# Two cross attentions and an MLP in float32: order of side work, earlier operands, and weight loads of full width

## The chip, the core and the metric

The kernel runs on one core of a Trainium2 chip, as one launch. The metric is the device time in microseconds, from the start of the program to its end; lower is better. All data and all arithmetic are float32.

## The reference

The input x has 8 batches of 100 rows and 512 columns, and the context has 8 batches of 361 keys and 512 columns. A first attention with one head and weights of its own (here called layer 0) adds to x. Two cross attentions over the same context follow (l = 0 and 1 in the code), each with 16 heads of 128, biases, and one extra bias key and bias value. Then comes an MLP with 2048 hidden columns.

```python
def _cross_attention(q_in, kv_in, wq, bq, wk, bk, wv, bv, wo, bo, bias_k, bias_v):
    qh = (q_in @ wq + bq).reshape(b, q_len, H, K)
    kh = (kv_in @ wk + bk).reshape(b, t, H, K)
    vh = (kv_in @ wv + bv).reshape(b, t, H, K)
    kh = jnp.concatenate([kh, jnp.broadcast_to(bias_k, (b, 1, H, K))], axis=1)
    vh = jnp.concatenate([vh, jnp.broadcast_to(bias_v, (b, 1, H, K))], axis=1)
    logits = jnp.einsum('bqhk,bthk->bhqt', qh, kh) / scale
    weights = jax.nn.softmax(logits, axis=-1)
    ctx = jnp.einsum('bhqt,bthk->bqhk', weights, vh).reshape(b, q_len, H * K)
    return ctx @ wo + bo
...
x = res + _cross_attention(_layer_norm(x, ...), xf_1, ...)
...
return x + jax.nn.gelu(h @ w_fc1 + b_fc1, approximate=False) @ w_fc2 + b_fc2
```

## The kernel before, in words

**The algebra.** The keys are never formed. A head's queries are multiplied by the transposed key weights (`wide_queries`, L677), so that 16 heads of 100 rows make 1600 rows of 512 columns for each batch, in the tile `Z`. These rows are multiplied with the transposed context (scores), and the probabilities with the context itself (mixes); the value weights come after that (`head_out`, L881), and then the output weights (`attn_out`, L944). The big products use a scheme that needs seven block products instead of eight, at the price of sums of blocks that are formed beside them.

**Steps.** For each of the two attentions the batches go in pairs (q = 0 to 3), and the 1600 rows in three groups (g = 0 to 2). That makes 24 steps, and each has two halves, j = 0 and 1, one for each batch of the pair. In group 0 the first 64 rows are a tile of their own (`lone_tile`, L687 to L698); all other rows go in pairs of 128 row tiles (`pair_part`, L730, in four parts). Part 1 of a pair writes the score of the bias key into the probabilities on GpSimd (L755). The bias key's scores come from `bias_scores` (L627): four products of `E`, which has 16 columns for each block of 128 channels, with the normalised rows.

**What is formed beside the products.** `pair_sums` (L700 to L707) forms four sums of `Z` on GpSimd for one pair, in the tile `sums`, which has two buffers. VectorE transposes the probabilities in 32 by 32 blocks (`turned`, L354) into the tile `pT`, at a lower priority. When a group is turned, `column_sums` (L790) forms four sums of its blocks on GpSimd. The mixes (`mixed`, L831) use them so: blocks 0, 6 and 5 in part 0, blocks 7, 3 and 5 in part 1, blocks 1, 2 and 4 in part 2, blocks 8 and 4 in part 3. `bias_probs` (L866) fetches the probabilities of the bias key back from memory, broadcast to all partitions, into the tile `pb`, which has one buffer; `head_out` scales them on GpSimd (L878) and adds them on VectorE (L888). `weight_sums` (L903) forms sums of the output weights on GpSimd while l is 0 and q is odd. `bias_keys` (L606) makes `E` of the second attention while l is 0 and q is 2: two broadcasts by SP into a tile `h`, a subtraction on GpSimd (L611), and eight multiplications with accumulation on VectorE (L599) over the query weights. For the first attention the same is done in layer 0, with the VectorE instructions pinned to the program's order. The tile `h` has two buffers; the rows that are to be normalised (`load_rows`, L366, then L575) use it too.

**The order of the work.** A list of units is written out. Each step's score units, in groups, get a "fill" between them: projections for the next step, mixes of the half before, head products of the step before, output products, sums of weights. A unit names the weight blocks that it needs; rings of buffers (six slots in "w", two in "v") issue the loads by SP in the order of first use, as soon as the slot is free. A scheduler then gives every engine its queue, by the priority of the place in the list and by readiness in its own model of time; each engine runs its queue in order. `keep_in_program_order` keeps an instruction in its place.

The output units of a step begin with `bias_probs`, in the second half of the step after:

```python
res = [unit(lambda h=h: head_out(l, q, h), ("v", ("wv", l, q, h // 2))) for h in range(*WHOLE[g])]
return [unit(lambda: bias_probs(l, q, g))] + res
```

The sums for the next pair stand in part 1 of a pair (L1248), and the additions to the fill are these (L1287 to L1292):

```python
if l == 0 and q == 2:
    fill += e_units(1)[4 * k // 3 : 4 * (k + 1) // 3]
if l == 0 and q % 2:
    fill = woven(fill, sums_units(q // 2)[slice(*{0: (0, 2), 1: (2, 4), 2: (4, 6), 5: (6, 8)}.get(k, (0, 0)))])
if g == 1 and j and n < len(steps) - 2:
    fill.append(rows_unit((q + 1) % 4))
```

Of the kernel before, what the change touches and what calls it, by code (L numbers as in the profile page):

```python
# [18 lines left out]
P = 128  # L19
DT = D // P  # L20
# [59 lines left out]
def two_cross_attentions(ctx: ExitStack, tc: tile.TileContext, a: dict, out: bass.AP):  # L80
# [11 lines left out]
    def psum(pool, shape, name):  # L92
        return pool.tile(shape, F32, tag=pool.name, name=name)
# [110 lines left out]
    def unit(fn, *keys):  # L204
        return fn, keys
# [68 lines left out]
    ones = const.tile([P, 1], F32, tag="ones", name="ones")  # L274
    nc.gpsimd.memset(ones, 1.0)
    bqs = const.tile([P, 2, H], F32, tag="bqs", name="bqs")
    E = const.tile([P, 2, DT, H], F32, tag="E", name="E")
    e0 = const.tile([H, 2], F32, tag="e0", name="e0")
    half = const.tile([L, 1], F32, tag="half", name="half")
    nc.gpsimd.memset(half, -0.5)  # L280
# [313 lines left out]
    def bias_sums(l, p, dk, pinned):  # L594
        w = w4(("wqe", l, p))
        for c in range(DT):
            for h in range(2):
                wh = w[:, c, h * K : (h + 1) * K]
                ins = nc.vector.scalar_tensor_tensor(  # L599
                    wh, wh, 1.0 / math.sqrt(K), dk[:, h * K : (h + 1) * K], ALU.mult, ALU.mult,  # L600
                    accum_out=E[:, l, c, 2 * p + h : 2 * p + h + 1],
                )
                if pinned:
                    tc.keep_in_program_order(ins)

    def bias_keys(l, p):  # L606
        cols = slice(p * 2 * K, (p + 1) * 2 * K)
        dk = work.tile([P, 2, 2 * K], F32, tag="h", name=f"dk_{l}_{p}")
        broadcast(nc.sync, dk[:, 0, :], l, "bias_k", cols)
        broadcast(nc.sync, dk[:, 1, :], l, "bk", cols)  # L610
        nc.gpsimd.tensor_tensor(dk[:, 0, :], dk[:, 0, :], dk[:, 1, :], ALU.subtract)  # L611
        bias_sums(l, p, dk[:, 0, :], False)


    dk0 = [zf[:, i * 2048 : (i + 1) * 2048] for i in (3, 4)]
# [10 lines left out]

    def bias_scores(l, q):  # L627
        hT = hTs[l, q]
        ps = psum(ps_mm, [H, NQ], f"psb_{l}_{q}")
        for c in range(DT):  # L630
            nc.tensor.matmul(ps, E[:, l, c, :], hT[:, c, :], start=(c == 0), stop=(c == DT - 1))
        sT = work.tile([H, NQ], F32, tag="sT", name=f"sT_{l}_{q}", bufs=1)
        nc.vector.tensor_scalar(sT, ps, e0[:, l : l + 1], -1.0, ALU.add, ALU.mult)
# [65 lines left out]

# [90 lines left out]
    def column_sums(l, q, g, j, engine=nc.gpsimd):  # L790


        t, t3 = pTs[l, q, g, j], columns(l, q, g, j)
        nc.sync.dma_start(out=pbd[l, q * QB + j][:, slice(*ROWS[g])], in_=t3[TS : TS + 1, 2, :])
        engine.tensor_tensor(t[:, 6], t[:, 1], t[:, 0], ALU.subtract)  # L795
        engine.tensor_tensor(t[:, 1], t[:, 1], t[:, 3], ALU.subtract)
        engine.tensor_tensor(t[:, 7], t[:, 3], t[:, 6], ALU.subtract)  # L797
# [313 lines left out]
    W = "w"  # L1111
    steps = [(l, q, g) for l in range(2) for q in range(B // QB) for g in range(NG)]

    def e_units(l):

        return [unit(lambda p=p: bias_keys(l, p), (W, ("wqe", l, p))) for p in range(H // 2)]

    def project_units(n):
        l, q, g = steps[n]
# [30 lines left out]
    def out_units(n):  # L1150
        l, q, g = steps[n]
        res = [unit(lambda h=h: head_out(l, q, h), ("v", ("wv", l, q, h // 2))) for h in range(*WHOLE[g])]
        return [unit(lambda: bias_probs(l, q, g))] + res

    def rows_unit(q, tag="h"):

# [66 lines left out]
    def score_units(n, j):  # L1223
# [17 lines left out]
        for m, r in enumerate(pairs):  # L1241
            after = [r + 2 * P] if m == 0 else [pairs[0]] if j == 0 else []
            for part in range(4):
                u = [unit(lambda r=r, part=part: pair_part(l, q, j, r, part), key)]
                if part < 3:
                    n = (len(late) + 2 - part) // (3 - part)
                    u, late = late[:n] + u, late[n:]
                if part == 1:  # L1248
                    jj = j if m == 0 else j + 1
                    u += [unit(lambda x=x, jj=jj: pair_sums(l, q, jj, x)) for x in after]  # L1250
                res.append(u)
            late = end(r)
            res[-1], late = late[:1] + res[-1], late[1:]
# [5 lines left out]
    for n, (l, q, g) in enumerate(steps):  # L1259
        ahead = project_units(n + 1) if n + 1 < len(steps) else []  # L1260
        half_ahead = (len(ahead) + 1) // 2
        for j in range(QB):
# [10 lines left out]
            if n == len(steps) - 1:  # L1273
                outs = held[:4] if j == 0 else held[4:8]
            elif j and n:
                outs = out_units(n - 1)
                if n == len(steps) - 2:
                    held, outs = outs + out_units(n), []
            part = woven(part, outs) if len(part) > len(outs) else woven(outs, part)
            if mix:  # L1280
                lead = (len(part) + 2) // 3 if ahead else len(part) - 2 + j
# [3 lines left out]
            else:  # L1285
                fill += part
            if l == 0 and q == 2:  # L1287
                fill += e_units(1)[4 * k // 3 : 4 * (k + 1) // 3]
            if l == 0 and q % 2:
                fill = woven(fill, sums_units(q // 2)[slice(*{0: (0, 2), 1: (2, 4), 2: (4, 6), 5: (6, 8)}.get(k, (0, 0)))])  # L1290
            if g == 1 and j and n < len(steps) - 2:
                fill.append(rows_unit((q + 1) % 4))  # L1292
            groups = score_units(n, j)
            k = 0
            for i, us in enumerate(groups):
# [2 lines left out]
                units += fill[k:upto]  # L1298
                k = upto
    n = len(steps) - 1  # L1300
    drain = mix_units(n, 1) + out_units(n) + close_units(1, 1)
# [37 lines left out]
```

## Time and profile before

| What | us |
|---|---|
| Runs: median of 3 | 2037.32 |
| Runs: lowest and highest | 2035.34 and 2040.49 |
| The profiled execution: its time | 2032.83 |
| The profiled execution: its span | 2031.1 |
| TensorE clock granted, mean | 0.997 |
| Layer 0, 0 to 160 us: TensorE busy | 147.92 |
| First attention up to q = 2, 160 to 505 us: TensorE busy | 336.04 of 345 |
| q = 2 with E of the second attention, 505 to 730 us: TensorE busy | 217.17 of 225 |
| 730 to 1866 us: TensorE busy | 1112.92 of 1136 |
| The MLP, 1866 to 2031 us: TensorE busy | 157.44 of 165 |

An engine's busy time is the union of its instructions' records. TensorE has two rows: PE is the matmuls, PEld the loads of their stationary operand, which run beside the matmuls. In a row of the profile's timeline the first number is the start in us from the span's start, the second the duration, then the engine, the line, the operation, the tiles that are written and read, their shapes and how often in a row; in brackets is the engine's idle time before it and what ended that. The shape `128*64` of a load is rows by columns.

### The profile page before, as it was taken

The page shows a single profiled execution, that of the slowest core. Times are in us where ns is not written, and L with a number is a line of the kernel's source. Part 1 is how long each engine was busy: PE and PEld are TensorE (multiplying, and loading weights), DVE is VectorE, ACT ScalarE, POOL GpSimd, SP SyncE. Part 2 cuts the span into 40 slices and gives each one's busy share as a digit, 9 for nine tenths or more (in the row PEclk, how much of TensorE's full clock was granted, in tenths as well). Part 3 has the DMA queues.
Part 4 walks back from the last instruction along what each step waited for, and adds up shares of the span by engine and source line. Part 5 has one row for each costly group of instructions (what it writes and reads, how often), then busy time and mean ns, then how long its engine had stood idle before and what let it go on. Part 6 is the DMA issues. An engine that isn't in the chain of part 4 may idle for free.

```text
span 2031.1 us, 31457 instructions
## 1 busy us (share of the span) xinstructions
PE 1971.5 (97%) x10991; PEld 1799.4 (89%) x10991; DVE 1282.1 (63%) x3523; ACT 758.1 (37%) x2002; POOL 702.6 (35%) x1146
## 2 busy tenths in 40 slices
PE   9989999999999999999999999999999999999998
PEld 5668889998989888998999898989999999889998
DVE  2564766667666675666765765676666667665543
ACT  1324444444442334444432344444433444421231
POOL 3232432643344233444234323233243243325140
PEclk9999999999999999999999999999999999999999
DMA  8796224742645445534634353225334432135342
GB/s 253 255 313 201 83 80 134 219 135 75 195 125 159 135 125 185 180 105 128 205 117 130 114 169 111 94 73 170 97 114 128 133 124 82 56 105 167 116 128 71
DMA packets 250681, 283.87 MB, mean 140 GB/s; under 512 B 37608, under 2 KB 212108, under 8 KB 247196
## 3 DMA queue, kind: packets, MB, share of 16 engines
q1 hardware_dynamic: 246340, 271.51, 42.9%
q0 software_dynamic: 2112, 6.40, 0.9%
q10 hardware_dynamic: 2072, 3.97, 0.6%
q8 instruction: 87, 1.43, 0.3%
q14 instruction: 70, 0.57, 0.1%
HBM read 242.86 MB, written 38.97 MB: 139 GB/s over the span
## 4 chain that ended last, share of the span: by engine, by line
PE 75%; DVE 13%; ACT 4%; DMA 3%; POOL 2%; issue 2%; SPq 0%; DVEq 0%; POOLq 0%; ACTq 0%
PE sx L721 9%; PE mx L831 9%; PE pwo_P L944 7%; PE mz L831 7%; PE pq L661 7%; PE pqw L677 7%; DVE pT L354 6%; PE po L881 6%; PE sz L721 4%; PE my L831 3%; PE sy L721 2%; PE pfx L1084 2%; PE pgx L1035 2%; PE sc L474 2%; DVE wqe L599 2%
## 5 line engine op out<-in xcount | busy, mean ns | idle before, releaser
L354 DVE STREAM_TRANSPOSE pT<-p 32x192 f32<-32x192 f32 (+1 forms) x1664 | 602.2, 362 | 83.6 <-ACT p L338 53.7
L831 PE MATMUL mx<-pT,ctx 128*128 128x256 f32 (+3 forms) x960 | 283.0, 393 | 20.7 <-DVE Z L857 6.4
L721 PE MATMUL sx<-cT,Z 128*128 128x181 f32 x1152 | 230.0, 318 | 3.7 <-DVE p L761 3.7
L755 POOL TENSOR_SCALAR p<-nsb 128x1 f32<-128x1 f32 x192 | 37.4, 214 | 531.0 <-DVE pT L354 494.7
L831 PE MATMUL mz<-pT,ctx 105*128 105x256 f32 (+3 forms) x768 | 207.8, 393 | 9.5 <-POOL pT L795 8.4
L721 PEld LDWEIGHTS sx<-cT,Z 128*128 128x128 f32 x1152 | 195.2, 191 | 17.0 <-DVE p L761 5.6
L831 PEld LDWEIGHTS mx<-pT,ctx 128*128 128x128 f32 (+1 forms) x960 | 169.4, 190 | 44.2 <-POOL pT L797 9.5
L677 PE MATMUL pqw<-q,wkT 128*128 128x200 f32 x1024 | 195.6, 334 | 0.0
L881 PE MATMUL po<-Z,wv 128*128 128x200 f32 x1024 | 194.1, 333 | 1.6 <-DMA wv<-in_L_xattn_wv_dram 1.6
L661 PE MATMUL pq<-hT,wq 128*128 128x200 f32 x1024 | 193.7, 333 | 0.0
L775 ACT ACTIVATE p<-p,nm 128x362 f32<-128x362 f32 x192 | 114.8, 598 | 187.6 <-DVE nm L774 185.1
L677 PEld LDWEIGHTS pqw<-q,wkT 128*128 128x128 f32 x1024 | 177.5, 191 | 5.4 <-issue 0.5
L881 PEld LDWEIGHTS po<-Z,wv 128*128 128x128 f32 x1024 | 175.0, 190 | 7.4 <-DMA wv<-in_L_xattn_wv_dram 2.2
L831 PEld LDWEIGHTS mz<-pT,ctx 128*128 128x128 f32 (+1 forms) x768 | 143.8, 191 | 42.0 <-POOL pT L795 12.3
L661 PEld LDWEIGHTS pq<-hT,wq 128*128 128x128 f32 x1024 | 175.1, 190 | 4.2 <-issue 1.4
L774 DVE TENSOR_REDUCE nm<-p 128x1 f32<-128x362 f32 x192 | 101.5, 529 | 102.1 <-ACT p L766 92.2
L721 PE MATMUL sz<-cT,sums 128*128 128x181 f32 x768 | 150.2, 318 | 1.1 <-ACT p L749 1.1
L704 POOL TENSOR_TENSOR sums<-Z 128x256 f32<-128x256 f32 x96 | 69.8, 727 | 231.8 <-ACT Z L680 158.1
L680 ACT COPY Z<-pqw 128x400 f32<-128x400 f32 x256 | 122.3, 489 | 69.5 <-PE pqw L677 69.3
L338 ACT ACTIVATE p<-p,rden 128x362 f32<-128x362 f32 (+2 forms) x216 | 129.0, 599 | 34.6 <-DVE rden L337 34.6
L721 PEld LDWEIGHTS sz<-cT,sums 128*128 128x128 f32 x768 | 125.3, 190 | 1.7 <-ACT p L749 1.7
L831 PE MATMUL my<-pT,ctx 128*128 128x256 f32 (+3 forms) x384 | 102.5, 388 | 0.0
(379 smaller groups left out, 3112.6 us busy)
## 6 DMA issues: line engine op xcount, KB each, us to landing
wv<-in_L_xattn_wv_dram SPq DMA_DIRECT2D x64, 512.0 KB
wq<-in_L_xattn_wq_dram SPq DMA_DIRECT2D x64, 512.0 KB
wkT<-wkd SPq DMA_DIRECT2D x48, 512.0 KB
cT<-cTd SPq DMA_DIRECT2D x16, 1267.0 KB
wo_S<-wod SPq DMA_DIRECT2D x32, 512.0 KB
f<-in_L_xattn_w_fc_dram SPq DMA_DIRECT2D x32, 512.0 KB
wo_A<-in_L_xattn_wo_dram SPq DMA_DIRECT2D x24, 512.0 KB
xr<-xd SPq DMA_DIRECT2D x45, 200.0 KB
```

The costliest lines, as they stand in the source:

```text
L338: nc.scalar.mul(p[:rows, :n], p[:rows, :n], rden[:rows])
L354: nc.vector.transpose(dst[keys, :, :, i, :], src[i * QD : (i + 1) * QD, :, :, quarter, :])
L661: nc.tensor.matmul(ps, w[:, c, (h % 2) * K : (h % 2 + 1) * K], hTs[l, q][:, c, :], start=(c == 0), stop=(c == DT - 1),)
L677: nc.tensor.matmul(ps[:, c, :], w[:, h % 2, cc * P : (cc + 1) * P], qs[h], start=True, stop=True)
L680: nc.scalar.copy(Z[:, 2 * c2 : 2 * c2 + 2, :, h * L : (h + 1) * L], ps.rearrange("p c (b t) -> p c b t", b=QB),)
L704: nc.gpsimd.tensor_tensor(t[:, 0], a2[:, :2, :], a2[:, 2:, :], ALU.add)
L721: nc.tensor.matmul(ps[:, :KH], st["a"][a][:, c, :], st["ct"][:, blk, c, :], start=(first and c == 0), stop=(c == 1), skip_group_check=not ...
L774: nc.vector.tensor_reduce(nm, p[:, :S1], AX.X, ALU.max, negate=True)
L775: nc.scalar.activation(p[:, :S1], p[:, :S1], AF.Exp, bias=nm, accum_out=den)
L831: nc.tensor.matmul(ps, cx[:w, blk, :], pT[:w, u, :], start=first, stop=last, skip_group_check=more)
L881: nc.tensor.matmul(ps, w[:, c, (h % 2) * K : (h % 2 + 1) * K], Z[:, c, :, h * L : (h + 1) * L], start=(c == 0), stop=(c == DT - 1),)
L944: nc.tensor.matmul(ps, w[:, h, :], OB[i, j][:, h, :], start=(h == 0 and not more), stop=(h == 7), skip_group_check=more)
```

## The change

The parts are independent of each other in the code.

1. `E` becomes one row of 240 numbers for each partition: `E` of the second attention, `E` of the first, and zeros. A product of `bias_scores` loads 128 columns, the 16 wanted ones and what lies after them; only the first 16 rows of the result are read. A lone tile loads 128 columns of `Z` for 64, and only 64 rows of its result are read.
2. In `column_sums` the subtraction for block 7 comes before that for block 1.
3. `pair_sums` for the next pair stands in part 0 of a pair.
4. `bias_keys` is split: the two broadcasts (`bias_fetched`) are joined to a unit in the middle of the fill and name the weight block there; the subtraction and the VectorE sums stay at the fill's end, and the sums are pinned.
5. `bias_probs` is joined to a unit at three quarters of the fill of the step's first half, so it comes before the second half; the last two steps keep it where it was.
6. The two row loads are joined to a unit at three quarters of the fill.
7. Before the two sums of output weights in a fill stand two empty units that name the same weight blocks.

```diff
-    E = const.tile([P, 2, DT, H], F32, tag="E", name="E")
+    ef = const.tile([P, 2 * DT * H + P - H], F32, tag="E", name="E")
+    nc.gpsimd.memset(ef[:, 2 * DT * H :], 0.0)
+    E = [ef[:, (1 - l) * DT * H : (2 - l) * DT * H].rearrange("p (c h) -> p c h", c=DT) for l in range(2)]
...
-    def bias_keys(l, p):
+    dks = {}
+
+    def bias_fetched(l, p):
         cols = slice(p * 2 * K, (p + 1) * 2 * K)
-        dk = work.tile([P, 2, 2 * K], F32, tag="h", name=f"dk_{l}_{p}")
+        dks[p] = dk = work.tile([P, 2, 2 * K], F32, tag="h", name=f"dk_{l}_{p}")
         broadcast(nc.sync, dk[:, 0, :], l, "bias_k", cols)
         broadcast(nc.sync, dk[:, 1, :], l, "bk", cols)
+
+    def bias_keys(l, p):
+        dk = dks.pop(p)
         nc.gpsimd.tensor_tensor(dk[:, 0, :], dk[:, 0, :], dk[:, 1, :], ALU.subtract)
-        bias_sums(l, p, dk[:, 0, :], False)
+        bias_sums(l, p, dk[:, 0, :], True)
...
-        ps = psum(ps_mm, [H, NQ], f"psb_{l}_{q}")
+        ps = psum(ps_mm, [P, NQ], f"psb_{l}_{q}")
         for c in range(DT):
-            nc.tensor.matmul(ps, E[:, l, c, :], hT[:, c, :], start=(c == 0), stop=(c == DT - 1))
+            e = ef[:, ((1 - l) * DT + c) * H :][:, :P]
+            nc.tensor.matmul(ps, e, hT[:, c, :], start=(c == 0), stop=(c == DT - 1))
...
-        both = work.tile([P, 2, LONE], F32, tag="sums", name=f"both_{l}_{q}_{j}")
-        nc.gpsimd.tensor_tensor(both, Z[:, :2, j, :LONE], Z[:, 2:, j, :LONE], ALU.add)
+        both = work.tile([P, 2, P], F32, tag="sums", name=f"both_{l}_{q}_{j}")
+        nc.gpsimd.tensor_tensor(both, Z[:, :2, j, :P], Z[:, 2:, j, :P], ALU.add)
...
-        plain_scores(sc, rings["cT"].tiles["cT", l, q * QB + j], Z[:, :2, j, :LONE], Z[:, 2:, j, :LONE], both)
+        plain_scores(sc, rings["cT"].tiles["cT", l, q * QB + j], Z[:, :2, j, :P], Z[:, 2:, j, :P], both)
...
         engine.tensor_tensor(t[:, 6], t[:, 1], t[:, 0], ALU.subtract)
+        engine.tensor_tensor(t[:, 7], t[:, 3], t[:, 6], ALU.subtract)
         engine.tensor_tensor(t[:, 1], t[:, 1], t[:, 3], ALU.subtract)
-        engine.tensor_tensor(t[:, 7], t[:, 3], t[:, 6], ALU.subtract)
...
+    def sums_part(l, k):
+
+        n = {0: 0, 1: 1, 2: 2, 5: 3}.get(k)
+        if n is None:
+            return []
+        us = sums_units(l)[2 * n : 2 * n + 2]
+        return [unit(lambda: None, *us[0][1]), unit(lambda: None, *us[1][1])] + us
...
-                if part == 1:
+                if part == 0:
                     jj = j if m == 0 else j + 1
                     u += [unit(lambda x=x, jj=jj: pair_sums(l, q, jj, x)) for x in after]
...
-                fill += e_units(1)[4 * k // 3 : 4 * (k + 1) // 3]
+                for fetch, sums_ in e_units(1)[4 * k // 3 : 4 * (k + 1) // 3]:
+                    at = len(fill) // 2
+                    fill[at] = both_of(fill[at], fetch)
+                    fill.append(sums_)
...
+            if n and j == 0 and n < len(steps) - 1:
+                (fn, keys), (early, _) = fill[len(fill) * 3 // 4], probs_unit(n - 1)
+                fill[len(fill) * 3 // 4] = unit(lambda fn=fn, early=early: [fn(), early()], *keys)
             if g == 1 and j and n < len(steps) - 2:
-                fill.append(rows_unit((q + 1) % 4))
+                at = len(fill) * 3 // 4
+                fill[at] = both_of(fill[at], rows_unit((q + 1) % 4))
```

More of the change, by code (lines that the diff above doesn't have):

```diff
@@ L600, in bias_sums @@
                     wh, wh, 1.0 / math.sqrt(K), dk[:, h * K : (h + 1) * K], ALU.mult, ALU.mult,
-                    accum_out=E[:, l, c, 2 * p + h : 2 * p + h + 1],
+                    accum_out=E[l][:, c, 2 * p + h : 2 * p + h + 1],
                 )
@@ L628, in bias_scores @@
         hT = hTs[l, q]
-        ps = psum(ps_mm, [H, NQ], f"psb_{l}_{q}")
+        ps = psum(ps_mm, [P, NQ], f"psb_{l}_{q}")
         for c in range(DT):
-            nc.tensor.matmul(ps, E[:, l, c, :], hT[:, c, :], start=(c == 0), stop=(c == DT - 1))
+            e = ef[:, ((1 - l) * DT + c) * H :][:, :P]
+            nc.tensor.matmul(ps, e, hT[:, c, :], start=(c == 0), stop=(c == DT - 1))
         sT = work.tile([H, NQ], F32, tag="sT", name=f"sT_{l}_{q}", bufs=1)
-        nc.vector.tensor_scalar(sT, ps, e0[:, l : l + 1], -1.0, ALU.add, ALU.mult)
+        nc.vector.tensor_scalar(sT, ps[:H], e0[:, l : l + 1], -1.0, ALU.add, ALU.mult)
         nsb = work.tile([P, QB, 13], F32, tag="nsb", name=f"nsb_{l}_{q}")
@@ L1112, in two_cross_attentions, with both_of @@
     steps = [(l, q, g) for l in range(2) for q in range(B // QB) for g in range(NG)]
+    def both_of(u, v):
+        return unit(lambda: [u[0](), v[0]()], *(u[1] + v[1]))
     def e_units(l):
-        return [unit(lambda p=p: bias_keys(l, p), (W, ("wqe", l, p))) for p in range(H // 2)]
+        ks = [(W, ("wqe", l, p)) for p in range(H // 2)]
+        return [(unit(lambda p=p: bias_fetched(l, p), ks[p]), unit(lambda p=p: bias_keys(l, p), ks[p])) for p in range(H // 2)]
     def project_units(n):
@@ L1152, in out_units, with probs_unit @@
         res = [unit(lambda h=h: head_out(l, q, h), ("v", ("wv", l, q, h // 2))) for h in range(*WHOLE[g])]
-        return [unit(lambda: bias_probs(l, q, g))] + res
+        return [unit(lambda: None)] + res
+    def probs_unit(n):
+        l, q, g = steps[n]
+        return unit(lambda: bias_probs(l, q, g))
     def rows_unit(q, tag="h"):
@@ L1277, in two_cross_attentions @@
                 if n == len(steps) - 2:
-                    held, outs = outs + out_units(n), []
+                    held, outs = outs + [probs_unit(n)] + out_units(n)[1:], []
             part = woven(part, outs) if len(part) > len(outs) else woven(outs, part)
@@ L1287, in two_cross_attentions @@
             if l == 0 and q == 2:
-                fill += e_units(1)[4 * k // 3 : 4 * (k + 1) // 3]
+                for fetch, sums_ in e_units(1)[4 * k // 3 : 4 * (k + 1) // 3]:
+                    at = len(fill) // 2
+                    fill[at] = both_of(fill[at], fetch)
+                    fill.append(sums_)
             if l == 0 and q % 2:
-                fill = woven(fill, sums_units(q // 2)[slice(*{0: (0, 2), 1: (2, 4), 2: (4, 6), 5: (6, 8)}.get(k, (0, 0)))])
+                fill = woven(fill, sums_part(q // 2, k))
+            if n and j == 0 and n < len(steps) - 1:
+                (fn, keys), (early, _) = fill[len(fill) * 3 // 4], probs_unit(n - 1)
+                fill[len(fill) * 3 // 4] = unit(lambda fn=fn, early=early: [fn(), early()], *keys)
             if g == 1 and j and n < len(steps) - 2:
-                fill.append(rows_unit((q + 1) % 4))
+                at = len(fill) * 3 // 4
+                fill[at] = both_of(fill[at], rows_unit((q + 1) % 4))
             groups = score_units(n, j)
@@ L1300, in two_cross_attentions @@
     n = len(steps) - 1
-    drain = mix_units(n, 1) + out_units(n) + close_units(1, 1)
+    drain = mix_units(n, 1) + [probs_unit(n)] + out_units(n)[1:] + close_units(1, 1)
     norm, hid, mlp, end = mlp_units(0)
```

## The prediction

> **What bounds the kernel now.** I read the page's parts 1 and 2 first, then who waited for whom on TensorE, then the trace in order of time around each long wait. Part 1:
>
> ```profile
> PE 1971.5 (97%) x10991; PEld 1799.4 (89%) x10991; DVE 1282.1 (63%) x3523; ACT 758.1 (37%) x2002; POOL 702.6 (35%) x1146
> ```
>
> TensorE is the bound in every stage; nothing else is over 63%. So the change can only win time in which TensorE stands still or runs slowly. As the ends of matmuls are modelled, I took start to start times of neighbours: 154 ns for 181 columns, 169 for 200, 216 for 256, 242 for 288. What lies above these, summed over all 10,991 records (a matmul of this kernel is two of them), is about 86 us: 17 in layer 0, some 70 after it. That is all there is to win. The waits, of TensorE alone (total, times, longest):
>
> ```profile
> PE mz L831 <- POOL pT L795: 8.4, 9, 1.7
> PE mx L831 <- DVE Z L857: 6.4, 7, 2.0
> PE mx L831 <- ACT Z L840: 6.3, 4, 2.7
> PE mx L831 <- POOL pT L797: 5.3, 7, 0.9
> ```
>
> Two of the four are column_sums on GpSimd. Around 297 us it looks like this:
>
> ```profile
> 296.62 0.72 POOL L795 TENSOR_TENSOR pT<-pT 128x256 f32<-128x256 f32 x1 [0.85 <-DVE pT L354]
> 297.30 0.73 POOL L704 TENSOR_TENSOR sums<-Z 128x256 f32<-128x256 f32 x1
> 297.99 0.73 POOL L796 TENSOR_TENSOR pT<-pT 128x256 f32<-128x256 f32 x1
> 298.67 0.73 POOL L797 TENSOR_TENSOR pT<-pT 128x256 f32<-128x256 f32 x1
> ```
>
> TensorE wants block 7 (L797) second, but GpSimd makes block 1 (L796) before it and a pair sum (L704) between. The third place is the layer's second half, 505 to 760 us, where E of layer 1 is formed on VectorE:
>
> ```profile
> 569.57 0.29 DVE L599 SCALAR_TENSOR_TENSOR wqe<-wqe,dk 128x128 f32<-128x128 f32 x1 [5.34 <-DMA wqe<-in_L_xattn_wq_dram]
> ```
> ```profile
> 570.60 0.88 PE L721 MATMUL sx<-cT,Z 128*128 128x181 f32 x4 [1.65 <-DVE p L761]
> ...
> 575.05 1.74 PE L831 MATMUL mx<-pT,ctx 128*128 128x256 f32 x4 [1.95 <-DVE Z L857]
> ```
>
> VectorE stands 5.34 us before weights that haven't landed, with L761 and L857 queued behind; TensorE stands twice for it. And then its clock drops (the stretch, its length, PE busy, clock):
>
> ```profile
> 575.40:578.80 3.40, 3.40 (x12) 0.50 0.23 82
> 579.00:583.00 4.00, 4.00 (x24) 1.00 0.42 112
> 708.50:711.90 3.40, 3.40 (x11) 0.50 0.67 237
> ```
>
> Twelve matmuls in 3.4 us against 24 in 4.0. Last, the narrow weights (weight loads of one lone tile):
>
> ```profile
> 175.18 1.73 PEld L474 LDWEIGHTS sc<-cT,Z 128*64 128x64 f32 x12 [0.24 <-issue]
> ...
> 177.79 0.61 PEld L721 LDWEIGHTS sx<-cT,Z 128*128 128x128 f32 x4 [0.26 <-issue]
> ```
>
> The load isn't run ahead of the matmuls before it, on entering the 64 columns and on leaving them, and no semaphore is named.
>
> **What the Trainium skill says.** "TensorEngine Tiling (Array Packing)", Key Properties: "Changing tiling mode (not just tile) drains the TensorE"; its Available Configurations have column tiles of 64 and 32. The trace agrees: at 53 borders between a load of 64 or 16 columns and one of 128 the next matmul starts 86 to 95 ns late, and at the 100 column loads of layer 0 it doesn't. "TensorE: Matmul & The Clock Gate", What's actually happening: an idle window of about 3.4 us halves the clock; the trace has three such windows of 3.41 us inside the span, two of them right after these waits. The same page's table of specifications calls VectorE's and GpSimd's queues strict FIFO: L761 behind L599 above is that.
>
> **The change, part by part.**
>
> *Wide weights.* bias_scores loads 128 columns for 16, lone tiles 128 for 64. 53 borders of 91 ns vanish: **-4.8 us**, all on the path. Added: loads of 190 ns for 136 and 96. The rows sx (128 columns) and sc (64) both go at 153 to 154 ns per matmul, so they cost nothing while a matmul of 181 or 200 columns runs beside them. "both" (L694) grows from 454 to the 727 ns of L704, 16 x 0.27 = 4.4 us of GpSimd, which idles 65%; sc wants it only after twelve records (1.8 us). Without that cover at most 4.4 us. The zero fill at the start lies in GpSimd's 38 us wait. Bounds: 0 (if the pause isn't the width) to -4.8.
>
> *Block 7 before block 1.* L797 moves up by one operation, 0.69 us from start to start. TensorE's excess put down to L797 is 6.8 us in 11 places: one each of 1.08 (269 us), 1.07 (299), 1.08 (498), 1.07 (929), 1.07 (1353), 0.5 (1730), 0.5 (1816) and four of about 0.1. Taking up to 0.69 from each: 5 x 0.69 + 2 x 0.5 + 0.4 = 4.9. What is late next is block 1 (M3), 0.69 us behind block 7; M2 and the two z products stand between, six records of 0.216, 1.3 us, so it isn't late. Where the pair sum goes out of the way as well, the rest goes too. I take **-4.9**; bounds -3.5 and -6.8.
>
> *Pair sums at part 0.* L704 to L707 (2.9 us of GpSimd) go ahead of the two L755, which wait for VectorE's transposes 72 times, 494.7 us in all. At 206 us L755 waits 7.22 us, then three sums run, then L795, and TensorE loses 1.19 us: that goes. At 722 (1.25) and 1728 (1.86) the first sum waits for ScalarE's copy of Z, which this edit doesn't hasten; at 239, 297, 496, 926 and 1351 L795 itself waits for transposes. Queued behind the sums now: L755 and column_sums, if Z isn't copied yet. **-1.2**; bounds -4 and +3.
>
> *Layer 1's E (bias_fetched, bias_keys).* Sixteen broadcasts and eight weight loads of SP are asked for half a fill (some 15 us) earlier; eight GpSimd subtractions (0.73) and 64 VectorE sums stay, at the fill's end and pinned. The wait at 569 cost 1.81 + 2.11 + 0.15, plus half of a 3.41 us window, 1.7: 5.8. The burst of L599 at 703 to 706 cost 2.84 + 1.7 = 4.5; bursts at 740 to 760 1.5. The row loads' wait (4.24 us of VectorE at 765, 3.4 of TensorE) hangs on a free buffer, and I leave it. The first goes, half of the others: **-8**; bounds -12 and +10 (the third rival).
>
> *Rows, bias probabilities and output weights earlier.* Rows: two loads of 200 KB in SP's queue a quarter of a fill earlier. Probabilities: GpSimd's 42.7 us of waits for pb go, save the last two (9.9, 4.1), which aren't moved; but no long wait of TensorE that I followed back passes through L878, so 0. The two loads now sit in SP's queue before wq, wkT and wv; should pb's single buffer not be free, these wait too (SP waited 68.3 us for L888 in 13 places). Weight sums: 24.1 us of GpSimd waits go, and a wor block holds one of six weight slots half a fill longer; TensorE waits for no wq, wkT or wo now, and its worst wait for wv is 0.8 us. **0** for the three; bounds -2 and +3.
>
> Sum: 4.8 + 4.9 + 1.2 + 8 = 18.9. The order of the queues is made anew by a scheduler, so other queues meet elsewhere; of some 70 us of waits a twentieth, 3.5 us, may come back. **-15.4 us**. The profiled execution took 2032.8 us (span 2031.1, 1.7 around it), the median of the runs is 2037.3; a saving on TensorE holds for both, so I take it from the median: **2022 us**, and a profile near 2018.
>
> **The rivals.**
>
> *The waits come back elsewhere.* Only widths and block order count (9.7), and moved sums and bursts cost 5 to 6: **2033 us**. For it: VectorE has 1282 us of work, and most long waits end in a run of transposes; against it: the 5.34 us wait is for a load alone.
>
> *The pause isn't the width.* Then 4.8 stays: **2027 us**. For it speaks only that "issue" is named, not a cause; against it the 100 column loads, which show none.
>
> *Slower: pinned sums hold VectorE.* Eight groups of L599 now stand at a fixed place, behind GpSimd's subtraction, which stands behind L755. One such wait of 5.34 us costs TensorE 3.9 us (1.81 + 2.11). Eight cost 31, less the 8.4 that today's sums cost (3.4 of lost clock apart) and 10.9 of the other parts: +12, **2049 us**. It decides from five groups on (19.6 against 19.3). Against it: the fetch is half a fill ahead, and GpSimd waited at most 4.95 us for a broadcast just issued.
>
> *All of it works*, the interleaved sums and the row loads too: 4.8 + 6.8 + 1.2 + 11.8 + 3.4 = 28, **2009 us**.
>
> **How the numbers follow.** Chances: forecast 0.52, waits come back 0.20, width 0.08, slower 0.07, all 0.13. A measurement tells about 0.3% (6 us) from no change. Faster than 2031: the forecast, all, width, and a third of the second, 0.80; slower than 2043: 0.06; the rest 0.14. The range 2008 to 2035 reaches from the best case to the waits that come back, and leaves out the slower case and the tails of these two.
>
> **What would show it.** Loads of 64 and 16 columns gone and no pause of 91 ns around sc and psb; L797 waits under 2 us; no half clock at 575 and 708; VectorE never over 2 us before L599. Wrong would be: VectorE idle before L599 on the subtraction, new waits of sx or mx on L761 or L857, or TensorE waiting for wq or wkT loads.

## The result, and the profile after

| What | us |
|---|---|
| Before: median of 5 runs | 2037.32 |
| After: median of 5 runs | 2016.07 |
| After: lowest and highest | 2015.62 and 2020.65 |
| After, the profiled execution: time and span | 2018.84 and 2017.0 |

The ratio of after to before is 0.9906, with a 95% interval of 0.9892 to 0.9921: 19 us less (16 to 22). The ratio isn't the quotient of the two medians, which lie 21.3 us apart; where the two differ I use the ratio. The two profiled executions lie 14.0 us apart (2032.83 and 2018.84), their spans 14.1. The lines of the kernel after have moved: L354 is L358 now, L599 is L603, L721 is L731, L755 is L765, L761 is L771, L795 to L797 are L805 to L807 (block 7 at L806, block 1 at L807), L831 is L841, L840 is L850, L857 is L867, L575 is L579.

Part 1 of the page of after:

```profile
PE 1963.9 (97%) x10991; PEld 1814.2 (90%) x10991; DVE 1276.8 (63%) x3523; ACT 757.4 (38%) x2002; POOL 707.2 (35%) x1147
```

The work of the engines is the same to 1%, so what was won is time in which TensorE stood or ran slowly. Who waited for whom on TensorE after (total, times, longest):

```profile
PE mx L841 <- DVE Z L867: 6.6, 7, 2.1
...
PE mz L841 <- POOL pT L805: 4.9, 6, 1.0
...
PE ph L582 <- DVE xr L579: 4.0, 1, 4.0
...
PE mx L841 <- ACT Z L850: 2.3, 2, 1.6
...
PE mx L841 <- POOL pT L806: 1.2, 5, 0.3
```

Block 7 went from 5.3 to 1.2 us, the first sum (L805) from 8.4 to 4.9, ScalarE's copy of Z (L850) from 6.3 to 2.3. VectorE's Z (L867) is unchanged at 6.6 against 6.4, and a row is new: ph, the transposes of normalised rows, waits once, 4.0 us. GpSimd around the place that was shown at 297 us, in the trace of after:

```profile
294.40 0.73 POOL L805 TENSOR_TENSOR pT<-pT 128x256 f32<-128x256 f32 x1
295.09 0.34 POOL L765 TENSOR_SCALAR p<-nsb 128x1 f32<-128x1 f32 x2
295.39 0.73 POOL L806 TENSOR_TENSOR pT<-pT 128x256 f32<-128x256 f32 x1
296.07 0.73 POOL L807 TENSOR_TENSOR pT<-pT 128x256 f32<-128x256 f32 x1
```

Between the first sum (L805) and block 7 (L806) stand only two short writes of the bias key's score (L765); the pair sums have gone ahead of both. The weight loads of the lone tile at 175 us:

```profile
175.42 1.90 PEld L478 LDWEIGHTS sc<-cT,Z 128*128 128x128 f32 x12
...
177.90 0.65 PEld L731 LDWEIGHTS sx<-cT,Z 128*128 128x128 f32 x4
```

128 columns, and the idle time in brackets is gone on entering and on leaving. VectorE's sums for E between 500 and 800 us (the group's busy time, the mean of one, the idle time before):

```profile
L603 DVE SCALAR_TENSOR_TENSOR wqe<-wqe,dk 128x128 f32<-128x128 f32 x64 | 18.0, 345 | 0.2
```

VectorE waits 0.2 us before them in all, where it waited 11.0 for the 64 sums of before. The clock, at the place of 575 us and at two new ones (a half clock is a stretch in which TensorE is granted half of its full clock; the columns are stretch, its length, PE, PEld, DVE, ACT and POOL busy, clock, DMA share and GB/s):

```profile
575.40:578.80 3.40, 3.40 (x20) 3.13 (x19) 1.85 (x5) 2.30 (x7) 0.00 (x0) 1.00 0.43 114
692.50:695.90 3.40, 3.40 (x11) 3.14 (x10) 3.22 (x9) 0.37 (x1) 0.71 (x3) 0.50 0.24 82
...
713.00:716.40 3.40, 3.40 (x12) 3.04 (x13) 1.34 (x4) 0.37 (x1) 3.32 (x6) 0.50 0.65 196
```

The half clock at 575 is gone; the one at 708 has become two, each behind a stand of TensorE, a time without a matmul (2.1 us before the first, 4.0 before the second). The second stand is the new row of the waits. On TensorE, VectorE and SP it looks like this:

```profile
708.27 0.62 PE L841 MATMUL mx<-pT,ctx 128*128 128x256 f32 x2
712.87 0.70 PE L582 MATMUL ph<-ident,xr 100*128 100x100 f32 x3 [3.98 <-DVE xr L579]
```
```profile
708.79 0.08 DVE L603 DVE_READ_ACCUMULATOR wqe<-wqe,dk 128x1 f32 x1
...
712.27 0.55 DVE L579 TENSOR_SCALAR xr<-xr,mv,rstd 100x512 f32<-100x512 f32 x1 [0.69 <-DVE pT L358]
```
```profile
708.93 0.31 SPq L370 DMA_DIRECT2D xr<-xd  x1
```

The row load leaves 0.06 us after the last sum for E has been read out (708.79 + 0.08): both use the tile `h`, and the pinned sums kept its buffer. The load and seven transposes follow, then L579, and TensorE has the transposes of these rows next in its queue.

Where the time went, by what TensorE's start to start times lie above those without a wait (the measure of the prediction; all excesses over 30 ns, the half clock in the rows where it falls; the prediction put the total of before at about 86, by this count it is 91.8):

| Cause, by the lines of before | before, us | after, us |
|---|---|---|
| borders of 64, 16 and 128 columns | 4.8 | 0 |
| mx on block 7 (L797) | 6.8 | 2.0 |
| mz on the first sum (L795) | 9.9 | 5.9 |
| mx on ScalarE's Z (L840) | 7.0 | 2.7 |
| mx on VectorE's Z (L857) | 8.5 | 9.2 |
| sx on VectorE's p (L761) | 4.5 | 4.1 |
| sx on ScalarE's p (L746) | 4.4 | 6.8 |
| mz on ScalarE's Z (L843) | 2.4 | 5.3 |
| ph on VectorE's rows (L575) | 0 | 4.1 |
| sc on ScalarE's cT, in layer 0 | 0 | 4.0 |
| pd on ScalarE's xc, in layer 0 | 4.6 | 1.5 |
| all causes, these and smaller ones | 91.8 | 78.0 |

The total falls by 13.8, near the 14.1 between the spans. In layer 0, which the change hardly touches, one wait went and another of like size came (the last two rows of causes).

### The profile page after: what moved, and what is told of

Its sections match the earlier page's. It is cut to its first block, busy times and chain, and to the rows that moved or that the text cites. A ratio compares the mean times of both kernels' runs of the same rounds, so it can differ in the third digit from the quotient of the medians.

```text
span 2017.0 us, 31494 instructions
## 1 busy us (share of the span) xinstructions
PE 1963.9 (97%) x10991; PEld 1814.2 (90%) x10991; DVE 1276.8 (63%) x3523; ACT 757.4 (38%) x2002; POOL 707.2 (35%) x1147
## 4 chain that ended last, share of the span: by engine, by line
PE 79%; DVE 10%; DMA 4%; ACT 3%; issue 2%; POOL 1%; SPq 0%; DVEq 0%; ACTq 0%; POOLq 0%
PE sx L731 9%; PE mx L841 9%; PE mz L841 7%; PE pq L671 7%; PE pqw L687 7%; PE po L891 7%; PE pwo_P L954 6%; DVE pT L358 5%; PE sz L731 5%; PE my L841 3%; PE sc L478 2%; PE sy L731 2%; PE pfx L1094 2%; PE pgx L1045 2%; DMA xr<-xd 1%
## 5 line engine op out<-in xcount | busy, mean ns | idle before, releaser
L358 DVE STREAM_TRANSPOSE pT<-p 32x192 f32<-32x192 f32 (+1 forms) x1664 | 602.1, 362 | 84.3 <-ACT p L342 54.5
L841 PE MATMUL mx<-pT,ctx 128*128 128x256 f32 (+3 forms) x960 | 281.3, 391 | 11.2 <-DVE Z L867 6.6
L731 PE MATMUL sx<-cT,Z 128*128 128x181 f32 x1152 | 229.6, 318 | 3.2 <-DVE p L771 3.1
L841 PE MATMUL mz<-pT,ctx 105*128 105x256 f32 (+3 forms) x768 | 208.3, 393 | 7.3 <-POOL pT L805 4.9
L731 PEld LDWEIGHTS sx<-cT,Z 128*128 128x128 f32 x1152 | 195.2, 191 | 16.6 <-DVE p L771 5.2
L765 POOL TENSOR_SCALAR p<-nsb 128x1 f32<-128x1 f32 x192 | 39.1, 223 | 477.6 <-DVE pT L358 421.4
L841 PEld LDWEIGHTS mx<-pT,ctx 128*128 128x128 f32 (+1 forms) x960 | 170.0, 190 | 30.6 <-DVE Z L867 6.8
L841 PEld LDWEIGHTS mz<-pT,ctx 128*128 128x128 f32 (+1 forms) x768 | 144.0, 191 | 40.9 <-ACT Z L853 8.1
L731 PE MATMUL sz<-cT,sums 128*128 128x181 f32 x768 | 149.3, 316 | 0.7 <-ACT p L759 0.7
L731 PEld LDWEIGHTS sz<-cT,sums 128*128 128x128 f32 x768 | 124.8, 189 | 1.0 <-ACT p L759 1.0
L841 PE MATMUL my<-pT,ctx 128*128 128x256 f32 (+3 forms) x384 | 102.5, 388 | 0.0
```

Of the source, the lines that this page charges most:

```text
L358: nc.vector.transpose(dst[keys, :, :, i, :], src[i * QD : (i + 1) * QD, :, :, quarter, :])
L731: nc.tensor.matmul(ps[:, :KH], st["a"][a][:, c, :], st["ct"][:, blk, c, :], start=(first and c == 0), stop=(c == 1), skip_group_check=not ...
L841: nc.tensor.matmul(ps, cx[:w, blk, :], pT[:w, u, :], start=first, stop=last, skip_group_check=more)
```

## The experiments

The parts have the numbers that they have in the section on the change. Each kernel was run in turn with the kernel before; a ratio is to that, with its 95% interval. Beside the ratio I set the two traces against each other by steps: how much earlier or later than in the trace of before each of the 24 steps starts. That tells where a part wins or loses, which one sum of a profile doesn't, since half clocks fall in other places from one execution to the next. A step starts with the first score product of its first pair; in the trace of before the steps of q = 2 (6 to 8) start at 558, 628 and 717 us, step 9 at 791 and step 10 at 859 us. (The row for 505 to 730 us in the table ahead of the prediction covers q = 2 only roughly.)

**Part 1 alone.**

```diff
-        ps = psum(ps_mm, [H, NQ], f"psb_{l}_{q}")
+        ps = psum(ps_mm, [P, NQ], f"psb_{l}_{q}")
...
-        both = work.tile([P, 2, LONE], F32, tag="sums", name=f"both_{l}_{q}_{j}")
+        both = work.tile([P, 2, P], F32, tag="sums", name=f"both_{l}_{q}_{j}")
```

> The kernel before with the wide weights alone (part 1). Theory, the pause is the switch of the load's width: all 53 pauses of about 91 ns around sc and psb vanish and nothing else changes, 4.8 us less, a ratio of 0.9976. Rival, the pause is not the width: the pauses stay, ratio 1.000. Second rival, the scheduler makes other queues of it: the pauses go, but other waits of TensorE change by more than 2 us.

Measured: 2032.66 against 2035.51 us, ratio 0.9982 [0.9973, 0.9991], so 3.7 us. In its trace no excess is left at a border. Its span, 2032.8, shows no gain; this execution has five half clocks where the one of before has three, and at 1.7 us each the two explain 3.4 of the 5.4 us that are missing against the ratio. The pause is the width.

**Part 2 alone.**

```diff
         engine.tensor_tensor(t[:, 6], t[:, 1], t[:, 0], ALU.subtract)
+        engine.tensor_tensor(t[:, 7], t[:, 3], t[:, 6], ALU.subtract)
         engine.tensor_tensor(t[:, 1], t[:, 1], t[:, 3], ALU.subtract)
-        engine.tensor_tensor(t[:, 7], t[:, 3], t[:, 6], ALU.subtract)
```

> The kernel before with block 7 formed before block 1 alone (part 2). Theory: TensorE's excess at L797's place falls from 6.8 to about 1.9 us (what a pair sum between the two leaves), 4.9 us less, a ratio of 0.9976. Rival: block 1 is late next or the wait moves to the next mix, so that the ratio is within 0.999 to 1.001 though the wait at block 7 is gone.

Measured: 2031.4 against 2035.51, ratio 0.9978 [0.9971, 0.9986], 4.5 us. The excess at block 7 fell from 6.8 to 2.0, and no wait for block 1 came up in its place.

**Part 3 alone.**

```diff
-                if part == 1:
+                if part == 0:
```

> The kernel before with the pair sums in part 0 alone (part 3). Theory: the wait at 209 us (1.2 us) goes and little else moves, ratio about 0.9994. Rival: the sums, now ahead of L755 and of the column sums, hold these up: waits on L795 and on ScalarE's copies grow by 3 us or more, ratio 1.0015.

Measured: 2032.37 against 2035.51, ratio 0.9987 [0.9978, 0.9995], 2.6 us. The excess at the first sum (L795) fell from 9.9 to 7.9: the wait of 1.19 us behind the sums of 206 us is gone, and the one at 1728 fell from 1.85 to 1.14.

**Part 4 alone.**

```diff
-                fill += e_units(1)[4 * k // 3 : 4 * (k + 1) // 3]
+                for fetch, sums_ in e_units(1)[4 * k // 3 : 4 * (k + 1) // 3]:
+                    at = len(fill) // 2
+                    fill[at] = both_of(fill[at], fetch)
+                    fill.append(sums_)
```

> The kernel before with the split bias keys alone (part 4). Theory: the 5.3 us wait of VectorE at 569 us and the half clock after it go, the stretch from 505 to 630 us is 6 us shorter; then the row load that shares the buffers h waits for the pinned sums, and a stall of some 4 us with a half clock appears near 710 us, so that about 2 to 6 us stay, ratio 0.997 to 0.999. Rival, the pin itself holds VectorE: it stands before L599 for over 2 us in several of the eight groups and the ratio is above 1.

Measured: 2044.36 against 2035.51, ratio 1.0043 [1.003, 1.0056]: **slower** by 8.7 us. By steps, it wins 6.3 us between 558 and 628 us (the wait for weights at 569 is gone, as the forecast said) and loses 13.8 between 791 and 859. Of the stall that the forecast had near 710 a stand of 3.6 us came, at 720, but it ended with column sums on GpSimd (L800) and not with the rows, and from step 7 to step 9 the kernel gains 0.4 us all the same. In the place of the loss TensorE stands twice:

```profile
816.78 1.57 PE L726 MATMUL sx<-cT,Z 128*128 128x181 f32 x4 [4.01 <-DVE p L766]
826.83 2.07 PE L836 MATMUL mx<-pT,ctx 128*128 128x256 f32 x4 [5.58 <-DVE Z L862]
```

and each stand has a half clock with it, the first from 816.7 us on for 3.4 us, the other from 823.5 on for 6.8 (same columns as above):

```profile
816.50:819.90 3.40, 3.12 (x9) 2.76 (x10) 1.51 (x5) 1.80 (x5) 2.62 (x8) 0.53 0.83 244
...
823.50:830.30 6.80, 3.47 (x9) 2.65 (x10) 3.97 (x11) 1.96 (x6) 2.06 (x3) 0.50 0.54 160
```

VectorE's own waits from 787 to 830 us name the cause, the rows of layer 1's first pair:

```profile
DVE xr L575 <- DMA xr<-xd: 12.9, 2, 6.9
```

So VectorE does hold TensorE, but not before the sums, as my slower rival had it. And TensorE itself doesn't want these rows yet. It reads them a hundred microseconds later, for the transposes of layer 1:

```profile
929.33 0.51 PE L578 MATMUL ph<-ident,xr 100*128 100x100 f32 x4
```

The instruction that normalises the rows (L575) merely stands that early in VectorE's queue, ahead of the adds (L766, L862) for which TensorE waits. SP's queue shows why the rows are late (start, duration of the issue):

```profile
801.07 3.63 SPq L918 DMA_DIRECT2D wod<-wor  x2
804.76 0.62 SPq L876 DMA_DIRECT2D pb<-pbd  x1
805.42 2.52 SPq L138 DMA_DIRECT2D wor<-in_L_xattn_wo_dram  x4
...
808.50 0.43 SPq L876 DMA_DIRECT2D pb<-pbd  x1
808.97 0.37 SPq L366 DMA_DIRECT2D xr<-xd  x1
815.80 0.52 SPq L918 DMA_DIRECT2D wod<-wor  x1
...
819.72 0.55 SPq L366 DMA_DIRECT2D xr<-xd  x1
```

Both row loads (L366) stand behind stores of summed output weights (L918, `weight_sums`), which wait for GpSimd. In the trace of before the same two loads were gone long ago:

```profile
759.40 0.43 SPq L366 DMA_DIRECT2D xr<-xd  x1
...
760.32 0.36 SPq L366 DMA_DIRECT2D xr<-xd  x1
```

They left right after the last sum for E, which ended at 758.96. With part 4 the last two groups of sums, pinned at the end of the last half, run from 783.9 to 789.5, and the row loads, which take the same tile, come after them. Another way out, to place L575 later in VectorE's queue, has no run of its own; with parts 4 and 7, below, the second L575 comes later by itself, and its wait is gone.

**Parts 5, 6 and 7 alone** (probabilities, rows and weight blocks sooner; their lines of the diff, none of the others).

```diff
+            if n and j == 0 and n < len(steps) - 1:
+                (fn, keys), (early, _) = fill[len(fill) * 3 // 4], probs_unit(n - 1)
...
+                fill[at] = both_of(fill[at], rows_unit((q + 1) % 4))
...
+        return [unit(lambda: None, *us[0][1]), unit(lambda: None, *us[1][1])] + us
```

> The kernel before with the three earlier fetches alone: bias probabilities, rows, blocks of the output weights (parts 5, 6, 7). Theory: TensorE waits for none of them, so little moves: ratio 0.998 to 1.000 (GpSimd's waits for pb fall from 42.7 us to below 20). Rival: they are worth by themselves most of what the single parts leave unexplained, ratio 0.992 or less.

Measured: 2034.17 against 2034.66, ratio 0.9993 [0.9983, 1.0003]: nothing that can be told from zero. GpSimd's waits for `pb`, which were to fall from 42.7 us below 20, are 39.0 us, and those for the output weights rose from 24.1 to 41.3.

**All but part 4.**

```diff
-                for fetch, sums_ in e_units(1)[4 * k // 3 : 4 * (k + 1) // 3]:
-                    at = len(fill) // 2
-                    fill[at] = both_of(fill[at], fetch)
-                    fill.append(sums_)
+                fill += e_units(1)[4 * k // 3 : 4 * (k + 1) // 3]
```

> The changed kernel without part 4 (keys as before). Theory, part 4 is worth some 6 us in the whole although it costs 9 us alone: ratio 0.9935 to 0.9945 to the kernel before, and VectorE's wait for wqe near 565 us with the half clock is back. Rival, part 4 costs in the whole too: ratio 0.986 to 0.989, faster than the changed kernel.

Measured: 2021.9 against 2034.66, ratio 0.9936 [0.9922, 0.995]: 13 us, and the single parts make 3.7 + 4.5 + 2.6 + 1.4 = 12.2. VectorE's wait for weights and a half clock at 573 us are back (VectorE's waits from 500 to 800 us):

```profile
DVE wqe L603 <- DMA wqe<-in_L_xattn_wq_dram: 8.8, 2, 4.6
```

From 0.9936 to 0.9906 is part 4's worth in the whole: 6 us won, though it costs 9 alone. Something among the other parts takes its loss away.

**Parts 4 and 6** (the rows asked for sooner).

```diff
-                fill.append(rows_unit((q + 1) % 4))
+                at = len(fill) * 3 // 4
+                fill[at] = both_of(fill[at], rows_unit((q + 1) % 4))
```

> The kernel before with the split keys and the earlier rows (parts 4 and 6). Theory, the keys alone lost 14 us near 816 us because the pinned sums give the buffers h back late and the row loads then come last, behind other loads; with the rows asked for earlier these waits of VectorE before the rows (5.9 and 6.9 us) go, ratio 0.995 to 0.999. Rival, another part of the change (output weights or probabilities earlier) clears SP's queue there: the ratio stays near 1.004.

Measured: 2041.84 against 2034.66, ratio 1.0033 [1.0023, 1.0042]. My theory fell: the row loads still left at 809.1 and 819.4, and VectorE waited 5.4 and 6.4 us for them. A unit's place in the list isn't what holds them: they leave before step 10, in whose second half their unit stands, has begun (866 us in this trace).

**After, with the sums for E earlier.** The eight groups are given to the six halves as 1, 2, 2, 0, 1, 2 in place of 1, 1, 2, 1, 1, 2.

```diff
-                for fetch, sums_ in e_units(1)[4 * k // 3 : 4 * (k + 1) // 3]:
+                for fetch, sums_ in e_units(1)[slice(*((0, 1), (1, 3), (3, 5), (5, 5), (5, 6), (6, 8))[k])]:
```

> The changed kernel with no bias keys in the half in which the rows are loaded: the eight units go 1, 2, 2, 0, 1, 2 to the six halves instead of 1, 1, 2, 1, 1, 2. Theory, the stall of TensorE of 4.1 us at 713 us and the half clock after it (1.7) come from the second row waiting for a buffer h: they go, some 5 us less than the changed kernel, ratio 0.987 to 0.989. Rival, the two units in the second half cost as much on VectorE: ratio 0.990 or more.

Measured: 2011.49 against 2034.66, ratio 0.989 [0.9872, 0.9908], span 2009.2. The stand and the half clock at 713 us are gone: the second row load leaves at 689.9, not 708.9, and step 9 starts 16.3 us sooner than before, where after starts it 10.7 sooner. In the profile it is 7.8 us ahead of after, a part of it because this execution has one half clock where after's has three, one of double length. The intervals of the two ratios overlap at the edge, so that it beats after is likely and not shown.

**Parts 4 and 5, 4 and 7, and 4 to 7 together.** These ask what cures part 4. The edits are the lines of these parts, as above.

```diff
+            if n and j == 0 and n < len(steps) - 1:
+                (fn, keys), (early, _) = fill[len(fill) * 3 // 4], probs_unit(n - 1)
+                fill[len(fill) * 3 // 4] = unit(lambda fn=fn, early=early: [fn(), early()], *keys)
```

> Part 4 together with part 5 (the read-back of the turned probability rows queued earlier). With part 4 alone the row loads of layer 1's first pair went out at 809.0 and 819.7 us, each straight behind a read-back of turned rows (804.8, 808.5) and a set of output-weight blocks; in the full change both read-backs went out together, at 791.9 and 792.6, and both row loads at 798.2 and 798.8. Theory (the read-backs hold SyncE's queue): both row loads before 803 us, VectorE waits under 1 us before the square sums, the 14 us between 791 and 859 us are gone, and the ratio is 0.997 (6 us won at the weights' wait, nothing given back). Rival (the blocks of part 7 hold it, or the rows' unit of part 6): row loads still at 809 and 819, ratio 1.004.

```diff
+        us = sums_units(l)[2 * n : 2 * n + 2]
+        return [unit(lambda: None, *us[0][1]), unit(lambda: None, *us[1][1])] + us
```

> Part 4 together with part 7 (the output-weight blocks asked for sooner). Theory (the read-backs hold the queue): the row loads stay behind the read-backs, after 806 us, and the ratio stays at 1.003 to 1.005. Rival (the blocks hold it): row loads before 803 us, ratio 0.997.

```diff
+                (fn, keys), (early, _) = fill[len(fill) * 3 // 4], probs_unit(n - 1)
...
+                fill[at] = both_of(fill[at], rows_unit((q + 1) % 4))
...
+        return [unit(lambda: None, *us[0][1]), unit(lambda: None, *us[1][1])] + us
```

> Parts 4, 5, 6 and 7 together, without the wide loads, the order of use and the order of the pair sums. Theory (one of the fetch parts, or two together, clears the row loads): ratio 0.997, row loads before 803 us. Rival (parts 1 to 3 shift the work so that the loads fall otherwise): the waits near 815 us remain, ratio 1.003 or more.

| Kernel | ratio [95%] | row loads leave at | lost from step 9 to 10, us |
|---|---|---|---|
| part 4 | 1.0043 [1.003, 1.0056] | 809.0 and 819.7 | 13.8 |
| 4 and 6 | 1.0033 [1.0023, 1.0042] | 809.1 and 819.4 | 12.6 |
| 4 and 5 | 0.9994 [0.9984, 1.0004] | 809.8 and 810.4 | 4.6 |
| 4 and 7 | 1.001 [0.9996, 1.0025] | 810.4 and 822.0 | 4.8 |
| 4 to 7 | 0.996 [0.9946, 0.9974] | 799.4 and 800.0 | -0.6 |
| after | 0.9906 [0.9892, 0.9921] | 798.2 and 798.8 | -0.6 |

In the three kernels with part 7 the last column is too small by some 2.7 us: there 2.7 us of other products come between the lone tile of step 9 and its first pair, as they do in step 3, where no row load is late. Counted from the lone tile, they lose 7.5, 2.1 and 1.9 us, and the others what the table says.

Neither theory holds for one part. With 5 the two loads leave together, and VectorE waits 2.7 us; with 7 the second still leaves at 822.0, but VectorE waits for the first alone, 5.1 us: the second L575 stands later in its queue there, behind 16 transposes, and starts at 828.0, when its rows have landed. By these traces part 5 is worth 9 us here and part 7 some 6, and neither moves the first load. Of the sets that were run only 4 to 7 lets the loads leave in time, as they do in after; 4 with two of the three wasn't run. SP's queue with parts 4 to 7:

```profile
798.84 0.55 SPq L918 DMA_DIRECT2D wod<-wor  x1
799.43 1.24 SPq L366 DMA_DIRECT2D xr<-xd  x2
806.52 0.52 SPq L918 DMA_DIRECT2D wod<-wor  x1
```

Both loads now pass between two stores; VectorE waits 0.6 us for them.

**Part 4 with its last two groups sooner.** That is the loss undone at its source, with none of the other parts.

```diff
                 for fetch, sums_ in e_units(1)[4 * k // 3 : 4 * (k + 1) // 3]:
-                    at = len(fill) // 2
+                    at = len(fill) // (8 if k == 5 else 2)
                     fill[at] = both_of(fill[at], fetch)
-                    fill.append(sums_)
+                    fill.insert(len(fill) // 2 if k == 5 else len(fill), sums_)
```

> Part 4 alone, with one change: in the last half before layer 1 the two fetches stand at an eighth of the half's list and the two groups of sums in its middle, in place of the fetches in the middle and the sums at its end. In the kernel before, the last two groups of sums ran at 747 to 749 and 754 to 759 us and the two row loads, which take the same buffers, left at 759.4 and 760.3; with part 4 alone the groups ran at 782.0 to 789.5, and the loads left at 809.0 and 819.7, behind two stores of summed weight rows that waited for GpSimd. Theory (the late groups of sums hold the row loads' buffers): the last sums end before 775 us, both row loads leave before 790 us, VectorE waits under 1 us for them, and the 14 us between 791 and 859 us are gone: ratio 0.996 to 0.998. Rival (the loads stand behind the stores whatever frees the buffers): loads at 809 us or later, ratio 1.003 or more.

Measured: 2030.8 against 2035.79, ratio 0.9973 [0.9963, 0.9982], so 5.5 us won. The last sums ran from 762.8 to 766.6, and the row loads left a microsecond later (SP, then VectorE):

```profile
767.50 0.80 SPq L366 DMA_DIRECT2D xr<-xd  x2
```
```profile
774.06 1.23 DVE L575 TENSOR_SCALAR xr<-xr,mv,rstd 100x512 f32<-100x512 f32 x2
```

VectorE doesn't wait for them, and from step 9 to step 10 nothing is lost (-0.1 us). So part 4's loss was the late release of the tile `h` at the end of the last half, which put the row loads behind stores that wait for GpSimd. Moving two groups by some 22 us turned 8.7 us lost into 5.5 us won. (The edit moves their two fetches as well; that these alone did it is not excluded by this run, but the loads leave within a microsecond of the last sum, as they do in before and at 708.9 us in after.)

## Why the prediction was right, and where not

| Term | forecast, us | measured, us |
|---|---|---|
| wide weights | -4.8 | -3.7 (-5.5 to -1.8) |
| block 7 before block 1 | -4.9 | -4.5 (-5.9 to -2.8) |
| pair sums at part 0 | -1.2 | -2.6 (-4.5 to -1.0) |
| E of layer 1, alone | -8 | +8.7 (+6.1 to +11.4) |
| E of layer 1, in the whole | -8 | -6 (-10 to -2) |
| rows, probabilities, blocks, alone | 0 | -1.4 (-3.5 to +0.6) |
| all | -15.4 | -19 (-22 to -16); profiles -14.0 |

**Wide weights and block 7.** Both mechanisms and both sizes held: 53 borders of 91 ns went to none, which is what the Trainium skill, "TensorEngine Tiling (Array Packing)", Key Properties, led one to expect if a load of 64 or 16 columns counts as another tiling mode, which the page doesn't say, and the excess at block 7 fell by the forecast 4.8. What is left of it, 2.0 us, is five places of 0.4 at which one pair sum still stands between L805 and L806.

**Pair sums.** The one wait that I followed, at 206 us, went. The term may have been too small, though its 1.2 lies inside the measured interval: the waits for L795 fell by 2.0 us in all (9.9 to 7.9 with this part alone). Against the forecast the one at 1728 shrank too.

**E of layer 1.** The wait for weights at 569 and its half clock went, and with them 6.6 us between 558 and 628 us, as forecast. Two steps of this term failed. The first is "hangs on a free buffer, and I leave it": the row loads' buffer is the tile that the pinned sums hold, so the sums' new place sets when the rows can be fetched. That is the 13.8 us of part 4 alone (undone by moving two groups), and 4.1 us plus a half clock at 713 in after (gone when no sums stand in that half). The second is that I took "half of the others" for the bursts: the burst of 703 to 706 is still there, at 705.5 to 708.9, and the stand behind it is no longer the burst's but the rows'. The slower rival had the right engine and the wrong place: VectorE never stood before the sums (0.2 us), it stood before the rows, until 26 and 36 us after the last sum.

**Rows, probabilities and output weights.** "0 for the three" holds alone. In company it doesn't: with part 4 they turn a ratio of 1.0043 into 0.996, 17 us. I costed them where the trace of before was waiting, and there they did little: GpSimd's waits for pb, which were to go but for the last two, are 40.8 us in after (42.7 before), and those for the output weights 30.6 (24.1); why these stayed no run tells. Their worth lies in a wait that another part of the change makes. No sum over parts, each against the kernel before, can show that.

**The sum.** The terms added up because the loss of part 4 and its cure come in one change, and that was luck: the forecast had neither, and both are about as large as the whole of it. The profiles differ by 14.0 us, near the forecast 15.4; the ratio says 19. Much of the difference can be one of executions: the half clocks fall in other places, and in other numbers, from one to the next (three in the trace of before, three in after, one of them of 6.8 us, and one in the kernel with 1, 2, 2, 0, 1, 2 groups), and the profiled run of before, 2032.83, was faster than all five runs beside after. Of the 165 runs of the kernel before in the experiments, the nine with a mean granted clock of 0.999 took 2032.1 us in the median and the four with 0.993 took 2041.5. What decides where half clocks fall stands in the last section.

**The signs that I named.** Right: the narrow loads and pauses gone, L797's waits at 1.2 us, VectorE under 2 us before the sums, no wait for wq or wkT. Half right: no half clock at 575, but one at 713 and one at 692. The list of what would be wrong had TensorE's waits on L761, L857, wq and wkT, and not the wait for the rows that came.

## What to carry to other kernels

When an instruction is moved or pinned, list the buffers that it keeps and who takes them next, then follow that next user through its DMA queue and to the instruction that waits for it: the price of the move stands where that instruction has its place in its engine's queue, here 20 to 36 us after the last sum and a hundred before TensorE reads the result. A part that is worth nothing alone can be what makes another part pay, so parts of a change that touch one queue or one tile are to be costed together. And where a profile has a wait that "hangs on a free buffer", name the holder before leaving it.

## What the runs showed of the hardware

**VectorE beside GpSimd.** Of the 128 sums for E in after, 118 take about 0.28 us (up to 0.4), one takes 0.46 and nine take 0.80 to 0.86. In each of the ten long ones a GpSimd addition or subtraction of two tensors of 256 columns is under way as it starts, and it ends 0.15 to 0.2 us after that one (in the trace of before there are 20 long ones, one of 2.49 us with several GpSimd instructions in a row). One of them, GpSimd first, then VectorE:

```profile
707.94 0.77 POOL L717 TENSOR_TENSOR Z<-Z 128x256 f32<-128x256 f32 x1
```
```profile
708.05 0.80 DVE L603 SCALAR_TENSOR_TENSOR wqe<-wqe,dk 128x128 f32<-128x128 f32 x1
```

GpSimd's ends at 708.71, VectorE's at 708.85. So a long sum isn't a slower one; its length goes with what was left of GpSimd's instruction when it started. Those of a single column (the power for rstd, L382) lengthen no sum that starts beside them. I had costed both engines as if they ran freely beside each other.

**Half clocks lie on a grid.** In each of the 14 traces all half clocks begin at whole multiples of 3.413 us from each other (in before at 128.2, 575.4 and 708.5 us, 131 and 39 multiples apart), and they last one or two such windows. Where this grid lies against the program's start differs from one execution to the next (a start divided by 3.413 leaves 1.9 us in before and 3.0 in after). TensorE's idle time in one window of the grid goes with the clock of the next; as idle I count the time without a matmul, from 12 us after the start on. After a window at full clock, each of the 42 with 1.94 us or more of idle time was followed by a half clock, none of the 8080 with 1.61 or less, and 15 of the 35 between. After a window at half clock a second one followed the nine times when 0.79 us or more were idle, and none of the 57 times when it was 0.48 or less. Two windows of before, each with the next (the first number after the length is the time with a matmul; the clock is the third number from the end):

```profile
571.95:575.36 3.41, 1.46 (x8) 1.08 (x7) 2.06 (x10) 2.45 (x7) 2.87 (x6) 1.00 0.53 147
575.36:578.77 3.41, 3.41 (x12) 3.14 (x11) 2.67 (x8) 1.42 (x4) 0.73 (x1) 0.50 0.24 84
...
1725.67:1729.08 3.41, 1.72 (x9) 1.12 (x7) 1.71 (x6) 1.06 (x3) 3.33 (x6) 1.00 0.69 201
1729.08:1732.49 3.41, 3.06 (x16) 2.57 (x15) 0.60 (x2) 1.55 (x4) 1.27 (x2) 1.00 0.05 16
```

The first has 1.95 us idle and a half clock after it, the second 1.69 and none. With parts 4 and 7 alone the grid lies otherwise, the window over the same place (1727.6 to 1731.0) has 2.05 us idle, and a half clock follows. So about half a window of idle time is enough, in one stand or in several, and a stand that the grid cuts in two can go free. The Trainium skill, "TensorE: Matmul & The Clock Gate", What's actually happening, speaks of an idle window of about 3.4 us; the traces agree with the length of the window, but 1.94 us of idle time in it was always enough here. (The three windows of 3.41 us that the prediction counts are half clocks, not idle windows; in before the longest wait ahead of one was 2.7 us.)
